# A masked attention layer on one core: the last 16 steps cut as 256 queries by two key blocks, the last tails begun sooner

## The chip, the core and the metric

The kernel runs on one core of a Trainium2 chip. A core has a matrix engine (PE, with its weight loads listed as PEld), a vector engine (DVE), an activation engine (ACT), a general engine (POOL) and a queue engine that only starts transfers (SP). Each engine works through its own list of instructions in order; they meet at semaphores. SBUF is the on-chip memory with 128 partitions, PSUM the small memory into which PE writes. The metric is the device time of one execution in microseconds (us), lower is better.

## The reference

Input `x` is (8, 2048, 256): 8 graphs of 2048 nodes with 256 channels. `adj` is one 2048 x 2048 adjacency matrix for all graphs. For each graph (H = 8 heads of D = 32):

```python
q, k, v = split(x @ w_qkv)                       # each (8, 2048, 8 heads, 32)
scores = einsum('fnhd,fmhd->fhnm', q, k) / sqrt(32)
attn = softmax(where(adj > 0, scores, -1e9), axis=-1)
t = einsum('fhnm,fmhd->fnhd', attn, v)
u = layernorm(x + t, ln1_g, ln1_b)
h = relu(u @ w1 + b1)
w = layernorm(u + h @ w2 + b2, ln2_g, ln2_b)
out = layernorm(x + w)                            # no gain, no shift
```

All of it is float32.

## The kernel before

**Steps.** The work is cut into 1024 items `(f, qc, g, mb)`: graph f (8), chunk of 512 queries qc (4), group of four heads g (2), block of 128 keys mb (16). Sixteen items with the same (f, qc, g) are a group. The main loop (L606) takes one step per item. In step t the program writes, in this order: what the planner has to fill in (`advance`), the exponential of item t+1 (`exponentials`, ACT), the scores of item t+2 (`scores`: four matmuls on PE into two PSUM tiles, then two additions of the mask on DVE, L233, which also move the scores to SBUF), the product of item t with V (`values`, four matmuls on PE, L249, summed in PSUM over the group), and what becomes of the finished tile p of item t (`add_up`). So DVE works about one item ahead of ACT, and ACT one ahead of PE's second product. "Step t" in this document means the 1024 items in order, 0 to 1023, and T(t) is the time at which L249 of item t starts. The last graph is steps 896 to 1023, the last group 1008 to 1023.

**PSUM.** Three score tiles in rotation, two of them for each item, hold the scores; two more banks hold the running product of a group and whatever the planner fills in. PE can write the scores of an item only when DVE has emptied the tile.

**Softmax sums.** The sum over keys is taken by adding p tiles: in a group POOL adds those of blocks 3, 6, 8, 10, 12, 14 into block 0 (L271), accumulating transfers started by POOL (L268) add others, and the four tiles left go through PE with a matrix of ones (`denominator`, L315). For the last group `denominator` starts three steps before the end and takes eight tiles.

**Tails.** When the two head groups of a query chunk are done, `outcome` transposes the products and divides them by the sums (`divide`, L356), adds x by an accumulating transfer that POOL starts (L340), and starts `tail`: `norm`, `feed_forward` (transposes, two matrix products, L54), `norm`, multiplication by the gain and addition (POOL, L368 and L370), a second accumulating transfer of x (L373), `norm`, and the store (SP). `norm` is four statistics instructions with their aggregates on DVE (L278, L279), four small instructions on POOL that end with the bias `nb` (L283 to L287), and four scalings on ACT (L290). Its argument `per` says how many of the four are put into one step; it is 1 for all tails but the last two. In the last graph the tails of chunks 0 and 1 begin at `begin + 10`, where `begin` is six steps after the chunk's last item.

**Planner.** Each piece of filling is a Python generator that yields at the points where it may be put off; `start(t, gen, due)` names the first step and the step at which it is due. The list is ordered by due step. Filling that needs PE asks for a PSUM bank (`BANK`), one at a time, and gets it when a credit, refilled in every step, is large enough or the piece is due; `MORE` holds the bank for another part and `WAIT` holds it idle. All of this happens when the program is built: on the chip each engine's order is fixed.

**The end.** After the last step the planner runs in its finishing mode: one request for a bank per round, the list still ordered by due step. `finish` (L443) takes the last chunk: `divide`, and then its rows in two halves (`half_rows`, L396), which take turns. What is still open of chunk 2's tail comes in between.

The planner's loop, which decides who gets the bank:

```python
        for e in list(fill):
            while e[2] is not None and e[0] <= t and e is not state["holder"]:
                if e[2] == BANK:
                    if not free or not more():
                        break
                    free = False
```

Of the kernel before, what the change touches and what calls it, by code (L numbers as in the profile page):

```python
# [16 lines left out]
ALU = mybir.AluOpType  # L17
# [44 lines left out]
def fast_path(ctx, tc, cst, x, adj, out, RS):  # L62
# [155 lines left out]


    PT, O, OT, RC, DT = {}, {}, {}, {}, {}  # L220

    def scores(item):
        f, qc, g, mb = item
        pt = PT[item] = pp.tile([P, 4, CH], F32, name="p")
        ps2 = [score_pair() for _ in range(2)]

        for half in (1, 0):
            for j in range(2):
                r = D * (2 * half + j)
                nc.tensor.matmul(ps2[half][:, j, :], KT[f, mb // TPC, g][r:r + D, (mb % TPC) * P:(mb % TPC + 1) * P],  # L230
                                 QT[f, qc, g][r:r + D, :], start=True, stop=True)
        for half, ps in enumerate(ps2):
            nc.vector.tensor_tensor(pt[:, 2 * half:2 * half + 2, :], ps,  # L233
                                    MK[f, qc, mb // 2][:, mb % 2, None, :].to_broadcast([P, 2, CH]), ALU.add)
# [6 lines left out]
    def values(item):  # L241
        f, qc, g, mb = item
        grp = (f, qc, g)
        if mb == 0:
            i = state["side"]
            O[grp] = ps_x[i].tile([P, CH], F32, name=f"x{i}")
        for h in range(4):
            r = D * h
            nc.tensor.matmul(O[grp][r:r + D, :], V[f, mb // TPC, g][:, mb % TPC, r:r + D], PT[item][:, h, :],  # L249
                             start=(mb == 0), stop=(mb == LAST))  # L250
        if mb == LAST:
            OT[grp] = op.tile([P, CH], F32, name=f"oT{g}")
            nc.scalar.copy(OT[grp], O.pop(grp))
# [6 lines left out]

    ENDED = MB - 5
    SUM = 4

    def add_up(item):
        f, qc, g, mb = item
        for chain in MOVED:
            if mb in chain[1:] and not ((f, qc, g) == items[-1][:3] and mb >= ENDED):
                nc.gpsimd.dma_start(PT[f, qc, g, chain[0]], PT.pop(item), accum_op=ALU.add)  # L268
        if mb in POOLED[1:] and not ((f, qc, g) == items[-1][:3] and mb >= ENDED):
            first = PT[f, qc, g, POOLED[0]]  # L270
            nc.gpsimd.tensor_tensor(first, first, PT.pop(item), ALU.add)  # L271


    def norm(t, per=1):
# [22 lines left out]
    def denominator(f, qc, g, ready):  # L297
        grp = (f, qc, g)
        blocks = [ALONE, MOVED[0][0], POOLED[0], MOVED[1][0]]
        late = {2: ready - 1, 3: ready}  # L300
        if (f, qc, g) == items[-1][:3]:
            blocks = [POOLED[0], 11, 12, MOVED[0][0], 13, 14, MOVED[1][0], 15]
            late = {n: len(items) - k for n, k in ((2, 2), (3, 1), (4, 1), (5, 0), (6, 0), (7, 0))}
        yield BANK
# [26 lines left out]
        begin = items.index((f, qc, g, LAST)) + SUM + 2  # L331
        start(begin, outcome(f, qc) if (f, qc) != (F - 1, NCK - 1) else finish(f, qc), begin)

    def outcome(f, qc):
# [3 lines left out]
        y = yp.tile([P, TPC, C], F32, name="y")  # L338
        yield from divide(f, qc, y)
        nc.gpsimd.dma_start(y, xin, accum_op=ALU.add)  # L340
        begin = items.index((f, qc, 1, LAST)) + SUM + 2
        if (f, qc) == (F - 1, NCK - 2):
            xb = take([P, TPC, C], F32)
            nc.sync.dma_start(xb, xin)
            start(begin + 8, tail(f, qc, y, xin, 2, xb), begin + 11)
        else:
# [13 lines left out]
    def tail(f, qc, y, xin, per=1, xb=None):  # L360
# [5 lines left out]
        z = y  # L366
        yield from norm(z, per)
        nc.gpsimd.tensor_tensor(z, z, rows(cst["g2r"]), ALU.mult)  # L368
# [26 lines left out]

    def half_rows(h, y, xr, xb, yT, hT, dst):  # L396
        own = slice(2 * h, 2 * h + 2)
        q = slice(2 * h * P, 2 * (h + 1) * P)
        y, xr, xb = y[:, own], xr[:, own], xb[:, own]

        def row2(v):
            return v[:, None, :].to_broadcast([P, 2, C])

        nc.vector.tensor_tensor(y, y, xr, ALU.add)
        if h:
            yield
        found = half_stats(y)
        yield
        half_norm(y, *found)
        nc.gpsimd.tensor_tensor(xr, y, row2(cst["g1r"]), ALU.mult)  # L410
        nc.gpsimd.tensor_tensor(xr, xr, row2(cst["be1b2r"]), ALU.add)  # L411
        yield
        ps = bank()
        transposes(ps, [y[:, j, a * P:(a + 1) * P] for a in range(2) for j in range(2)])
        for a in range(2):
            nc.scalar.activation(yT[:, a, q], ps[:, a * 2 * P:(a + 1) * 2 * P], AF.Identity,
                                 bias=cst["be1c"][:, a:a + 1], scale=cst["g1c"][:, a:a + 1])
        yield
        ps = bank()
        for d in range(2):  # L420
            for a in range(2):
                columns(ps[:, d * 2 * P:(d + 1) * 2 * P], w1s[:, a, d * P:(d + 1) * P], yT[:, a, q], start=(a == 0), stop=(a == 1))
            nc.scalar.activation(hT[:, d, q], ps[:, d * 2 * P:(d + 1) * 2 * P], AF.Relu, bias=cst["b1s"][:, d:d + 1], scale=1.0)  # L423
        yield
        ps = bank()
        for j in range(2):
            for d in range(2):
                columns(ps[:, j * C:(j + 1) * C], hT[:, d, (2 * h + j) * P:(2 * h + j + 1) * P], w2s[:, d, :],
                        start=(d == 0), stop=(d == 1))
        z = y  # L430
        nc.vector.tensor_tensor(z, ps.rearrange("p (b c) -> p b c", c=C), xr, ALU.add)
        found = half_stats(z)
        yield
        half_norm(z, *found)
        yield
        nc.vector.tensor_tensor(z, z, row2(cst["g2r"]), ALU.mult)  # L436
        nc.vector.tensor_tensor(z, z, xb, ALU.add)  # L437
        found = half_stats(z)
        yield
        half_norm(z, *found)  # L440
        nc.sync.dma_start(dst[:, own], z)

    def finish(f, qc):  # L443
        y = yp.tile([P, TPC, C], F32, name="y")
        xr, xb = state["rows"]
        yield from divide(f, qc, y)
        yT, hT = (work.tile([P, 2, CH], F32, name=n) for n in ("turned", "hT"))
        dst = out[f, qc * CH:(qc + 1) * CH, :].rearrange("(p j) c -> p j c", p=P)
        both = [half_rows(h, y, xr, xb, yT, hT, dst) for h in range(2)]
        while both:  # L450
            for e in list(both):
                if next(e, both) is both:
                    both.remove(e)
            yield 1

# [39 lines left out]
    def start(t, gen, due):  # L495
        fill.append([t, gen, 1, due])
        fill.sort(key=lambda e: e[3])
# [108 lines left out]
    for t, (f, qc, g, mb) in enumerate(items):  # L606
        if g == 1 and mb % 2 and (f + 1 < F or qc + 1 < NCK):
            load_mask(f + (qc + 1) // NCK, (qc + 1) % NCK, mb // 2)
        for what, *which in NEXT.get(t % FRAME, []):
            to = f if what is ask and which[0] else f + 1  # L610
            if to < F:
                at = (0, 0, 0) if what is turn else (which[0], 0, 0) if what is ask else (0, which[1], which[0] * TPC)
                start(t, what(to, *which), t + 3 * MB if what is turn else items.index((to, *at)) - LEAD - 1)
        if t == len(items) - MB // 2:
            xr, xb = state["rows"] = [take([P, TPC, C], F32) for _ in range(2)]
            nc.sync.dma_start(xr, x[f, qc * CH:(qc + 1) * CH, :].rearrange("(p j) c -> p j c", p=P))
        if t == len(items) - 2:
            nc.gpsimd.tensor_tensor(xb, xr, rows(cst["be2r"]), ALU.add)
# [14 lines left out]
        if mb == LAST and t + 1 < len(items):  # L633
            start(t + 2, denominator(f, qc, g, t + SUM), t + SUM + 4)
        if t == len(items) - 3:
            start(t, denominator(f, qc, g, t), t)
    t = len(items)
# [244 lines left out]
```

## Time and profile before

| what | value |
|---|---|
| median of three runs | 3190.41 us (3189.46 to 3194.38) |
| the profiled execution, whole | 3196.28 us |
| its span (first to last instruction) | 3194.5 us |
| busy share PE, DVE, POOL, ACT | 96%, 86%, 81%, 76% |
| last L249 starts, step 1023 | 3146.17 us |
| from there to the end of the span | 48.3 us |

The profile is one execution. Busy times add up the instructions of an engine; a line of the timeline gives start, length, engine, source line, operation, output and inputs, and in brackets how long the engine had been idle and what ended that. Where the timeline joins several records of one kind, `x8` says how many: a float32 matmul leaves two records, so the four matmuls of one `values` are x8. T(t) is found by counting the groups of L249 back from the last one. The profiled execution is 1.8 us longer than its span.

### The profile page before, as it was taken

How to read it: one execution, taken by the hardware profiler on the slowest of the kernel's cores; microseconds unless marked ns; L12 is line 12 of the kernel's file. 1: busy time of each engine (PE TensorE's matmuls, PEld its weight loads, DVE VectorE, ACT ScalarE, POOL GpSimd, SP SyncE). 2: the span in 40 equal slices, each digit the busy share in tenths (PEclk: the TensorE clock that was granted, in tenths of full speed). 3: DMA queues.
4: the chain of work that ended last, by engine and by line, in shares of the span. 5: the costliest groups of instructions: out<-in, count | busy, mean ns of one | idle time of the engine just before them, and what ended most of it. 6: DMA issues, size and time to landing. Idle time of an engine off the chain costs nothing. (4 is left out here: it accounts for less than half of the span.)

```text
span 3194.5 us, 68226 instructions
## 1 busy us (share of the span) xinstructions
PE 3081.7 (96%) x28868; PEld 963.0 (30%) x28868; DVE 2749.6 (86%) x3139; ACT 2417.7 (76%) x1909; POOL 2593.3 (81%) x1361
## 2 busy tenths in 40 slices
PE   7899999999999999999999999999999999999985
PEld 4222333222332223332333323323233233332222
DVE  4798988888889988889988988988988888889985
ACT  3677778777787777788777788778778778777774
POOL 0578888788888888888888888888889788889875
PEclk8899999999999999999999999999999999999998
DMA  9688889788798888898888899888879788888872
GB/s 323 142 192 193 183 175 199 161 188 189 179 195 188 191 194 178 176 204 196 187 177 174 194 208 198 168 182 196 196 174 203 177 196 192 176 177 166 178 150 64
DMA packets 153096, 589.46 MB, mean 185 GB/s; under 512 B 15024, under 2 KB 67760, under 8 KB 103888
## 3 DMA queue, kind: packets, MB, share of 16 engines
q0 software_dynamic: 64128, 433.22, 68.8%
q1 hardware_dynamic: 87840, 150.50, 13.7%
q8 instruction: 228, 3.74, 0.4%
q10 hardware_dynamic: 816, 1.31, 0.1%
q14 instruction: 84, 0.69, 0.1%
HBM read 146.67 MB, written 37.75 MB: 58 GB/s over the span
## 5 line engine op out<-in xcount | busy, mean ns | idle before, releaser
L233 DVE TENSOR_TENSOR p<-s,mask 128x1024 f32<-128x1024 f32 x2048 | 2409.1, 1218 | 325.0 <-PE s L230 182.9
L237 ACT ACTIVATE p<-p 128x2048 f32<-128x2048 f32 x1024 | 1956.0, 1910 | 566.5 <-DVE p L233 481.1
L271 POOL TENSOR_TENSOR p<-p 128x2048 f32<-128x2048 f32 x382 | 1875.4, 4909 | 359.1 <-ACT p L237 358.8
L230 PE MATMUL s<-qT,kT 32*128 32x512 f32 x8192 | 1172.5, 642 | 44.2 <-DVE p L233 39.4
L249 PE MATMUL x<-p,v 128*32 128x512 f32 x8192 | 1093.5, 606 | 4.6 <-ACT p L237 4.6
L230 PEld LDWEIGHTS s<-qT,kT 32*128 32x128 f32 x8192 | 320.9, 183 | 671.3 <-DVE p L233 643.6
L268 POOL DMA_DIRECT2D p<-p x382 | 416.8, 1092 | 70.1 <-ACT p L237 46.4
L249 PEld LDWEIGHTS x<-p,v 128*32 128x32 f32 x8192 | 161.5, 108 | 784.0 <-issue 310.2
L315 PE MATMUL x<-p,halves 128*32 128x512 f32 x2080 | 269.9, 595 | 0.0
L54 PE MATMUL x<-in,wqkv 128*32 128x512 f32 x1888 | 245.7, 592 | 0.0
L290 ACT ACTIVATE y<-y,nb,rs 128x256 f32<-128x256 f32 x372 | 219.1, 591 | 6.1 <-POOL nb L287 5.9
L278 DVE BATCH_NORM_STATS2 st<-y 128x6 f32<-128x256 f32 x372 | 155.0, 417 | 1.8 <-POOL y L370 1.8
L54 PE MATMUL x<-turned,w1s 128*32 128x512 f32 x992 | 123.9, 593 | 0.0
L54 PE MATMUL x<-w2s,hT 128*32 128x256 f32 x2016 | 121.8, 382 | 0.0
L54 PEld LDWEIGHTS x<-wqkv,in 128*32 128x32 f32 x3584 | 102.2, 110 | 64.1 <-issue 55.9
L54 PE MATMUL x<-wqkv,in 128*32 128x128 f32 x3584 | 117.4, 273 | 0.0
L315 PEld LDWEIGHTS x<-p,halves 128*32 128x32 f32 x2080 | 67.9, 111 | 156.9 <-issue 155.5
L368 POOL TENSOR_TENSOR y<-y,g2r 128x1024 f32<-128x1024 f32 x31 | 101.6, 3278 | 6.4 <-ACT y L290 6.4
L54 PEld LDWEIGHTS x<-in,wqkv 128*32 128x32 f32 x1888 | 61.3, 110 | 141.3 <-issue 116.5
L284 POOL TENSOR_TENSOR rs<-rs,mhalf 128x4 f32<-128x4 f32 x93 | 96.3, 1035 | 7.8
L370 POOL TENSOR_TENSOR y<-y,be2r 128x1024 f32<-128x1024 f32 x30 | 94.6, 3155 | 0.4
L54 PEld LDWEIGHTS x<-w2s,hT 128*32 128x32 f32 x2016 | 65.9, 111 | 70.7 <-issue 38.5
(121 smaller groups left out, 1301.1 us busy)
## 6 DMA issues: line engine op xcount, KB each, us to landing
p<-p POOLq DMA_DIRECT2D x382, 1024.0 KB, 10.0
in<-xd SPq DMA_DIRECT2D x87, 512.0 KB, 8.9
mask<-md SPq DMA_DIRECT2D x248, 128.0 KB, 8.6
y<-in_x_dram POOLq DMA_DIRECT2D x61, 512.0 KB, 10.1
p<-in_adj_dram SPq DMA_DIRECT2D x16, 1024.0 KB, 9.3
out_dram<-y SPq DMA_DIRECT2D x31, 512.0 KB, 6.2
in<-in_x_dram SPq DMA_DIRECT2D x30, 512.0 KB, 10.6
xd<-in SPq DMA_DIRECT2D x28, 512.0 KB, 8.8
```

Source lines behind the costliest of these rows:

```text
L54: nc.tensor.matmul(out[r:r + D], lhsT[:, r:r + D], rhs, start=start, stop=stop)
L230: nc.tensor.matmul(ps2[half][:, j, :], KT[f, mb // TPC, g][r:r + D, (mb % TPC) * P:(mb % TPC + 1) * P], QT[f, qc, g][r:r + D, :], start=Tr ...
L233: nc.vector.tensor_tensor(pt[:, 2 * half:2 * half + 2, :], ps, MK[f, qc, mb // 2][:, mb % 2, None, :].to_broadcast([P, 2, CH]), ALU.add)
L237: nc.scalar.activation(PT[item], PT[item], AF.Exp, scale=1.0 / math.sqrt(D))
L249: nc.tensor.matmul(O[grp][r:r + D, :], V[f, mb // TPC, g][:, mb % TPC, r:r + D], PT[item][:, h, :], start=(mb == 0), stop=(mb == LAST))
L268: nc.gpsimd.dma_start(PT[f, qc, g, chain[0]], PT.pop(item), accum_op=ALU.add)
L271: nc.gpsimd.tensor_tensor(first, first, PT.pop(item), ALU.add)
L278: nc.vector.bn_stats(st, t[:, j, :])
L284: nc.gpsimd.tensor_tensor(rs, rs, cst["mhalf"], ALU.pow)
L290: nc.scalar.activation(t[:, j, :], t[:, j, :], AF.Identity, bias=nb[:, j:j + 1], scale=rs[:, j:j + 1])
L315: nc.tensor.matmul(ps[r:r + D, :], cst["halves"][:, g, :], term[:, h, :], start=(n == 0), stop=(n == len(blocks) - 1))
L368: nc.gpsimd.tensor_tensor(z, z, rows(cst["g2r"]), ALU.mult)
```

## The change

The last group (`ENDING`) keeps its 16 steps, but a step takes 256 queries by two key blocks where it took 512 queries by one. The first eight steps finish the first 256 queries, the last eight the second 256. Scores, values and sums have their own branch for it: eight score matmuls of 256 columns in place of four of 512, the same two mask additions over the same number of elements, eight value matmuls of 256. Of each half's eight p tiles POOL adds two, one accumulating transfer adds a third, and five go through PE.

`closing(h)` replaces `finish`, `half_rows` and the special case of `denominator`: it takes the sums, the division and the whole tail of one half. It is started five steps into each half, `closing(0)` with due step 1024 and `closing(1)` with 1025, through the planner like other filling.

The other tails of the last graph are moved too. Chunks 0 and 1 begin at `begin + 7` in place of `begin + 10`, due at `begin + 18` in place of `begin + 26`, and put two statistics or scalings into a step where they put one; the second `norm` of the last graph's tails puts all four into one step. The multiplication by the second gain waits for step 15, 0 or 1 of a group (`CALM`). Chunk 2 adds x on DVE from the tile loaded by SP, in place of the accumulating transfer, and its tail begins at `begin + 3` in place of `begin + 8`.

```diff
+    ENDING = (F - 1, NCK - 1, 1)
+    HQ = CH // 2
     def scores(item):
...
+        if item[:3] == ENDING:
+            h, k = divmod(mb, MB // 2)
+            for b in range(2):
+                m = 2 * k + b
+                for half in (1, 0):
+                    for j in range(2):
+                        r = D * (2 * half + j)
+                        nc.tensor.matmul(ps2[half][:, j, b * HQ:(b + 1) * HQ],
+                                         KT[f, m // TPC, g][r:r + D, (m % TPC) * P:(m % TPC + 1) * P],
+                                         QT[f, qc, g][r:r + D, h * HQ:(h + 1) * HQ], start=True, stop=True)
...
     def add_up(item):
         f, qc, g, mb = item
+        if item[:3] == ENDING:
+            h = mb // (MB // 2) * (MB // 2)
+            if mb - h in (2, 4):
+                first = PT[f, qc, g, h]
+                nc.gpsimd.tensor_tensor(first, first, PT.pop(item), ALU.add)
+            elif mb - h == 3:
+                nc.gpsimd.dma_start(PT[f, qc, g, h + 1], PT.pop(item), accum_op=ALU.add)
+            return
+    CALM = (15, 0, 1)
     def outcome(f, qc):
...
-        yield from divide(f, qc, y)
-        nc.gpsimd.dma_start(y, xin, accum_op=ALU.add)
         begin = items.index((f, qc, 1, LAST)) + SUM + 2
         if (f, qc) == (F - 1, NCK - 2):
             xb = take([P, TPC, C], F32)
             nc.sync.dma_start(xb, xin)
-            start(begin + 8, tail(f, qc, y, xin, 2, xb), begin + 11)
+            yield from divide(f, qc, y)
+            yield 1
+            nc.vector.tensor_tensor(y, y, xb, ALU.add)
+            start(begin + 3, tail(f, qc, y, xin, 2, xb), begin + 18)
+            return
+        yield from divide(f, qc, y)
+        nc.gpsimd.dma_start(y, xin, accum_op=ALU.add)
+        if f == F - 1:
+            start(begin + 7, tail(f, qc, y, xin, 2), begin + 18)
         else:
             start(begin + 10, tail(f, qc, y, xin), begin + 26)
     def tail(f, qc, y, xin, per=1, xb=None):
...
-        yield from norm(z, per)
+        yield from norm(z, per if per == 1 else TPC)
+        while xb is None and f == F - 1 and state["now"] % MB not in CALM:
+            yield 1
+    def closing(h):
+        f, qc, g = ENDING
+        own, part, t0 = slice(2 * h, 2 * h + 2), slice(h * HQ, (h + 1) * HQ), len(items) - MB // 2 * (2 - h)
+        terms = [(5, 6), (1, 7), (0, 7), (6, 8), (7, 8)]
...
+        yield BANK
+        ps = bank()
+        for n, (block, when) in enumerate(terms):
+            if n:
+                yield MORE
+            while state["now"] < t0 + when:
+                yield WAIT
+            term = PT.pop((*ENDING, block + h * MB // 2))
+            state["credit"] -= 4 * CH
+            for b in range(2):
+                for i in range(4):
+                    r = D * i
+                    nc.tensor.matmul(ps[r:r + D, 0:HQ], cst["halves"][:, g, :], term[:, i, b * HQ:(b + 1) * HQ],
+                                     start=(n + b == 0), stop=(n + b == len(terms)))
+        dT = DT[f, qc]
+        nc.vector.tensor_tensor(dT[:, part], ps[:, 0:HQ], dT[:, part], ALU.add)
...
+        yield BANK
+        po = bank()
+        transposes(po, [OT[f, qc, gg][:, part][:, j::2] for gg in range(2) for j in range(2)])
...
+        for d in range(2):
+            yield BANK
+            ps = bank()
+            for a in range(2):
+                columns(ps[:, 0:HQ], w1s[:, a, d * P:(d + 1) * P], yT[:, a, part], start=(a == 0), stop=(a == 1))
...
-        if t == len(items) - 3:
-            start(t, denominator(f, qc, g, t), t)
+        for h in range(2):
+            if t == len(items) - MB // 2 * (2 - h) + 4:
+                start(t + 1, closing(h), len(items) + h)
```

The rest of `closing` is `half_rows` with the planner's yields (`BANK`, `MORE`, steps) between its parts, and the load of the last chunk's x, a single one in the order of the two halves, is moved to the start of the last group.

## The prediction

> **What bounds the kernel now.** I read the page first: the engines' busy shares and the groups with what ended their idle time.
>
> ```profile
> span 3194.5 us, 68226 instructions
> PE 3081.7 (96%) x28868; PEld 963.0 (30%) x28868; DVE 2749.6 (86%) x3139; ACT 2417.7 (76%) x1909; POOL 2593.3 (81%) x1361
> L233 DVE TENSOR_TENSOR p<-s,mask 128x1024 f32<-128x1024 f32 x2048 | 2409.1, 1218 | 325.0 <-PE s L230 182.9
> L230 PEld LDWEIGHTS s<-qT,kT 32*128 32x128 f32 x8192 | 320.9, 183 | 671.3 <-DVE p L233 643.6
> ```
>
> PE and DVE hand the score tiles to each other: the mask additions wait for PE's scores (182.9 us), the score loads for DVE to empty a tile (643.6 us). A step is as long as the longer of the two. The timeline of PE and DVE prices the steps of the last graph, as distances between starts of L249:
>
> - two mask additions and nothing else: 2.5 us;
> - with four more matmuls of 512 columns on PE: 2.92 us (here 2962.50 to 2965.42);
> - with twice that: 3.79 us;
> - with two statistics on DVE and no filling on PE: 3.33 us (3082.07 to 3085.40).
>
> ```profile
> 2962.50 1.06 PE L249 MATMUL x<-p,v 128*32 128x512 f32 x8
> 2963.38 1.04 PE L315 MATMUL x<-p,halves 128*32 128x512 f32 x8
> 2964.35 1.14 PE L230 MATMUL s<-qT,kT 32*128 32x512 f32 x8
> 2965.42 1.06 PE L249 MATMUL x<-p,v 128*32 128x512 f32 x8
> ...
> 3082.07 1.06 PE L249 MATMUL x<-p,v 128*32 128x512 f32 x8
> 3084.33 1.14 PE L230 MATMUL s<-qT,kT 32*128 32x512 f32 x8 [1.19 <-DVE p L233]
> 3085.40 1.07 PE L249 MATMUL x<-p,v 128*32 128x512 f32 x8
> ```
>
> A step that PE fills with four matmuls therefore has 0.42 us of room on DVE, about one statistics pair (0.42 us, L278). Two lie beyond the room, and so does a second lot of matmuls. That is the scale on which I weigh the moved tails.
>
> Then the timeline where the change works. At step 1009 ACT stood 5.60 us for POOL's `nb`, which sat behind an addition of two p tiles (5.43 us); PE then waited 4.64 us. Steps 1008 to 1011 took 3107.71 − 3091.67 = 16.04 us where three steps at 2.92 take 8.8.
>
> ```profile
> 3091.86 5.43 POOL L271 TENSOR_TENSOR p<-p 128x2048 f32<-128x2048 f32 x1
> 3099.06 0.19 POOL L287 TENSOR_SCALAR nb<-nb 128x4 f32<-128x4 f32 x1
> 3099.29 1.09 ACT L290 ACTIVATE y<-y,nb,rs 128x256 f32<-128x256 f32 x2 [5.60 <-POOL nb L287]
> 3102.23 1.60 PE L249 MATMUL x<-p,v 128*32 128x512 f32 x8 [4.64 <-ACT p L237]
> ```
>
> Last the end. The last product starts at 3146.17; 48.3 us follow. Of these PE is busy less than half up to 3170, at half clock between 3160 and 3170 (granted 0.50); the chain decides, not an engine.
>
> ```profile
> 3160.84 1.09 ACT L394 ACTIVATE y<-y,nb,rs 128x256 f32<-128x256 f32 x2 [11.99 <-issue]
> 3163.54 1.94 PE L54 MATMUL s<-turned,w1s 128*32 128x256 f32 x16 [0.66 <-ACT turned L416]
> 3171.32 3.38 PE L54 MATMUL x<-w2s,hT 128*32 128x256 f32 x32
> 3174.53 1.04 PE L54 MATMUL s<-turned,w1s 128*32 128x256 f32 x16
> ```
>
> **The change part by part.** The planner runs at build time, so I followed the changed program's order on each engine. It is the old one up to about step 939. I give the shift of T(t) against before, in the profiled execution's own time (3196.28 us whole, 5.87 above the median).
>
> *Chunk 0's first norm, three steps sooner: +4.9.* POOL starts the transfer that adds x at 2890.99; the page's group of that transfer has 10.1 us to landing, the two of the last graph 9.0 and 9.7. It lands at 2900.7. In the new order two statistics stand right behind the mask addition that ends at 2895.6, and the next addition, which ran at 2896.07, is queued behind them.
>
> ```profile
> 2890.99 0.87 POOL L340 DMA_DIRECT2D y<-in_x_dram  x1 [0.90 <-DVE y L356]
> 2893.22 2.36 DVE L233 TENSOR_TENSOR p<-s,mask 128x1024 f32<-128x1024 f32 x2 [0.27 <-PE s L230]
> 2896.07 2.36 DVE L233 TENSOR_TENSOR p<-s,mask 128x1024 f32<-128x1024 f32 x2 [0.50 <-PE s L230]
> 2899.00 2.36 DVE L233 TENSOR_TENSOR p<-s,mask 128x1024 f32<-128x1024 f32 x2 [0.57 <-PE s L230]
> ```
>
> It starts at 2900.7 + 0.95 = 2901.6, 5.5 late; PE waits for the tile, ACT for DVE. Two later statistics of before are already done (−0.6). Bounds: 3 (landing after 9.0, the 0.5 us gaps on DVE absorbed) to 5.5. Chunk 1 makes the same move without the wait: started at 2977.80 it lands by 2987.5, its statistics come at 2988.2.
>
> *The feed-forwards in lumps, steps 944 to 961: +3.5 (1 to 5).* Two steps with 8 matmuls of 512 and two with 16 of 256 take the place of eight with half as many: 4 × 3.79 + 4 × 2.5 = 25.2 against 8 × 2.92 = 23.4, +1.8. The second norm's four statistics fall into one step: 2.5 + 4 × 0.42 = 4.2 against four that each fitted beside 2.92: +1.3. Four scalings in one step (4 × 0.58 and an exponential of 1.91, 4.2 us) cost some 0.4, as ACT is ahead by most of a step.
>
> *Steps 961 to 976: +1.1 (0 to 2.5).* Chunk 1's first norm in pairs, one pair of 0.84 beyond the room, and a little more. *Steps 976 to 993: +2.4 (0.5 to 4).* Chunk 1's lumps (+1.8), its four statistics in a step, part of them beside PE.
>
> *Steps 993 to 1008: +4.7 (2.5 to 6.5).* Eight statistics in two lots (3.4) and chunk 2's addition of x, now on DVE (twice 512 elements, 0.68 each in L356: 1.3), minus the 0.42 that each of three filled steps has to spare: 3.4; before spent 1.7 there on its two steps of 3.33. Two steps running with four scalings each: 2 × (4 × 0.58 + 1.91) = 8.5 against 5.4, +3.1.
>
> *Steps 1008 to 1011: −7.2 (−8 to −5).* The gain's product now waits for a step of `CALM`, so the `nb` that was late comes at step 1002, not behind an addition of p. Nothing else is late there in the new order: four halves of 512 columns in each step, 2.92. This is the gain of the change.
>
> *The last group, steps 1011 to 1023: −1.2 (−3 to +2).* Before 38.46 us. After: twelve steps with PE filling at about 2.92 (w1s, w2s, then the first half's five sums), 35.0, plus four statistics in step 1017 (1.7) and 0.6 of ACT. The price of the 256-wide form is unknown: at one price per column it is nil, which the row supports (w2s at 256 is 382 ns, 512 wide 593 to 642, some 40 ns of it fixed); by 382 against half of 642 it would be 0.06 us × 8 records, 0.5 a step. The mask is cut into 256-element pieces; the same 1024 elements are charged.
>
> *The tail: +3.7 (−4 to +7).* In the order on PE only the first half's sums and one set of transposes stand before the last product. Behind it stand the first half's oT transposes, its y transposes, w1s, w1s, w2s, and only then the 40 matmuls of the second half's sums. Counted from T(1023): product 1.0, transposes to 1.7, two divisions, x, statistics (0.8 + 0.7 + 1.2) to 4.4, POOL's root and `nb` 1.6, scaling 1.1: 7.1. Transposes and the first `turned` to 9.5, w1s twice at the slow clock (1.94) to 13.4, hT 0.45, w2s at 3.38 to 17. The second half's sums, 40 × 0.12 = 4.8, to 22. Its sum, transposes, division and first norm take the same 6.4 as above: 28.4. From its transposes on I take what before shows for its second half, norm finished to the end: the w1s at 3174.53 to 3194.5 is 20.0, and 3.6 for transposes and `turned` ahead of it. 28.4 + 23.6 = 52.0 against 48.3.
>
> At the clock rule and trace meet. The row: after the 4.64 us of idling above the product took 1.60 instead of 1.06, and in the tail PE was slow from 3161.5 to about 3174.5, w2s in the middle included. The Trainium skill, TensorE: Matmul & The Clock Gate, Part 1, has full speed back after about 3.4 us of sustained work; by it w2s would already be fast, and the tail some 1.5 us shorter. I stay with the row, since its gaps will be in the new tail too.
>
> The other rule: the same page, section "LDWEIGHTS (loading the stationary operand)", prices a load by its columns, so 16 score loads of 128 columns in place of 8 would be 1.7 us, an estimate, against 1.14 of scores, and nine PE-filled steps some 5 us longer. The row says no: eight loads of 183 ns stand within 0.31 us, side by side.
>
> Sum: 4.9 + 3.5 + 1.1 + 2.4 + 4.7 − 7.2 − 1.2 + 3.7 = +11.9; 3196.28 + 11.9 = 3208.2, and as a median 3208.2 − 5.9 = 3202.3.
>
> **The rivals.**
>
> *The lumps hide (same).* If DVE and ACT are far enough ahead, what a lump costs in one step comes back in the next, and only the transfer, the stall that goes and the end count: 4.9 − 7.2 − 1.2 + 3.7 = +0.2, 3191. For it: ACT is 76% busy. Against: three score tiles let PE lead by less than a step, and the 3.33 us steps were not made up.
>
> *The first half really closes beside the steps (faster).* The mechanism is only in the tail. If the second half's sums don't stand behind the first half's feed-forward, its chain is sums to T+1, first norm at T+7.5, then 23.6: 31, 17 less than before; all in all about −9, 3181. It decides when those 40 matmuls start before T+8. Against: PE's order has them last.
>
> *A new wait for `nb` (slower still).* Two sets of `nb` in one step behind an addition of 4.55 us: ACT then waits at 991 or 1005 as it did at 1009. Price 3 to 5: 3207.
>
> That the change does nothing can hold only before step 939, where the order is the old one.
>
> **How the numbers follow.** About 0.2%, 6.4 us, is what a measurement of this kernel can tell from no change. Forecast 0.54 (own range 3194 to 3210), lumps hidden 0.20, new wait 0.17, first half closed 0.09. Same are the hidden lumps (0.17 of them) and the forecast's low end (0.04); faster is the closed half and the hidden lumps' low end (0.11); the rest is slower, 0.68. The range leaves out the closed half and the ends: 3187 to 3212.
>
> **What would show it.** Right: an idle stretch of about 5 us on DVE before statistics near 2896, ended by the transfer; T(1008) near 3108; no 5.60 us on ACT near step 1009; 40 matmuls of `halves` some 17 us after the last product; about 52 us from there to the end. Wrong: the sums of the second half directly behind the last product; the steps 944 to 1008 as long as before; a wait on `nb` in another place.

## The result and the profile after

The changed kernel took 3214.95 us (median of six, 3207.64 to 3220.71) against 3190.40 (median of six): 1.0072 times the time before, 95% interval 1.0052 to 1.0092. It is slower, as forecast, but the time lies above the range (3187 to 3212). The profiled execution took 3209.04 us, 0.8 from the forecast in its own time (3208.2). That nearness is an accident, as the stages below show.

The page of the changed kernel: the span, the engines, the groups that answer to those of before, and the groups of two waits.

```profile
span 3207.3 us, 68929 instructions
PE 3089.8 (96%) x29220; PEld 978.0 (30%) x29220; DVE 2757.6 (86%) x3146; ACT 2416.8 (75%) x1910; POOL 2588.5 (81%) x1358
L251 DVE TENSOR_TENSOR p<-s,mask 128x1024 f32<-128x1024 f32 x2016 | 2372.9, 1219 | 316.7 <-PE s L248 174.0
L248 PEld LDWEIGHTS s<-qT,kT 32*128 32x128 f32 x8064 | 316.6, 184 | 669.9 <-DVE p L251 643.8
L332 ACT ACTIVATE y<-y,nb,rs 128x256 f32<-128x256 f32 x372 | 217.3, 591 | 0.0
L320 DVE BATCH_NORM_STATS2 st<-y 128x6 f32<-128x256 f32 x372 | 154.8, 416 | 6.4 <-DMA y<-in_x_dram 5.1
```

The last two groups on the page of before:

```profile
L290 ACT ACTIVATE y<-y,nb,rs 128x256 f32<-128x256 f32 x372 | 219.1, 591 | 6.1 <-POOL nb L287 5.9
L278 DVE BATCH_NORM_STATS2 st<-y 128x6 f32<-128x256 f32 x372 | 155.0, 417 | 1.8 <-POOL y L370 1.8
```

Busy times have hardly moved. ACT's wait for `nb` is gone (5.9 us before, 0.0 now), and the statistics wait 5.1 us for a transfer that they did not wait for before.

The timeline says where. First PE and DVE at step 941, where chunk 0's first norm now stands:

```profile
2891.49 1.06 PE L282 MATMUL x<-p,v 128*32 128x512 f32 x8
2892.37 1.04 PE L54 MATMUL x<-in,wqkv 128*32 128x512 f32 x8
2898.53 2.09 PE L248 MATMUL s<-qT,kT 32*128 32x512 f32 x8 [5.12 <-DVE p L251]
2900.55 1.94 PE L282 MATMUL x<-p,v 128*32 128x512 f32 x8
...
2888.77 2.36 DVE L251 TENSOR_TENSOR p<-s,mask 128x1024 f32<-128x1024 f32 x2 [0.27 <-PE s L248]
2896.18 0.43 DVE L320 BATCH_NORM_STATS2 st<-y 128x6 f32<-128x256 f32 x1 [5.06 <-DMA y<-in_x_dram]
```

DVE stands 5.06 us for the transfer, PE 5.12 us for DVE; then the scores take 2.09 us in place of 1.14 and the product 1.94 in place of 1.06: the idle time cost PE its clock (granted 0.78 between 2890 and 2900). Next step 1001, DVE and POOL:

```profile
3078.85 2.35 DVE L251 TENSOR_TENSOR p<-s,mask 128x1024 f32<-128x1024 f32 x2
3081.11 5.00 DVE L384 TENSOR_TENSOR y<-y,in 128x1024 f32<-128x1024 f32 x1
3086.04 2.34 DVE L251 TENSOR_TENSOR p<-s,mask 128x1024 f32<-128x1024 f32 x2
...
3080.51 4.52 POOL L311 TENSOR_TENSOR p<-p 128x2048 f32<-128x2048 f32 x1 [0.29 <-ACT p L255]
```

L384 is the addition of x to chunk 2's tile, now on DVE. I had charged 1.3 us; it took 5.00, and ends 1.1 us after POOL's addition of two p tiles. Last PE after the last product (3158.74):

```profile
3160.30 0.75 PE L95 MATMUL x<-ident,oT 128*128 128x128 f32 x4 [0.49 <-ACT oT L275]
3165.74 1.39 PE L95 MATMUL x<-ident,y 128*128 128x128 f32 x4 [4.69 <-ACT y L441]
3167.79 3.64 PE L54 MATMUL s<-turned,w1s 128*32 128x256 f32 x32 [0.66 <-ACT turned L511]
3171.21 2.37 PE L54 MATMUL s<-w2s,hT 128*32 128x256 f32 x32
3173.40 4.49 PE L464 MATMUL x<-p,halves 128*32 128x256 f32 x80
...
3186.07 1.11 PE L95 MATMUL s<-ident,y 128*128 128x128 f32 x4
```

The second half's sums (L464) begin 14.7 us after the last product, behind the first half's feed-forward. The first half is not closed beside the steps.

### The profile page after: what moved, and what is told of

The parts are those of the page before. It is cut to its first block, busy times and chain, and to the rows that moved or that the text cites. A ratio compares the mean times of both kernels' runs of the same rounds, so it can differ in the third digit from the quotient of the medians.

```text
span 3207.3 us, 68929 instructions
## 1 busy us (share of the span) xinstructions
PE 3089.8 (96%) x29220; PEld 978.0 (30%) x29220; DVE 2757.6 (86%) x3146; ACT 2416.8 (75%) x1910; POOL 2588.5 (81%) x1358
## 4 chain that ended last, share of the span: by engine, by line
PE 83%; DVE 10%; DMA 2%; issue 2%; ACT 1%; POOL 1%; DVEq 0%; SPq 0%; ACTq 0%; POOLq 0%
PE s L248 31%; PE x L282 26%; PE x L54 16%; DVE p L251 7%; PE x L354 6%; PE x L95 3%; DMA in<-in_x_dram 1%; DVE st L320 1%; DVE dT L360 1%; PE s L236 0%; PE x L270 0%; POOL p L311 0%; DVE y L401 0%; DMA y<-in_x_dram 0%; ACT p L255 0%
## 5 line engine op out<-in xcount | busy, mean ns | idle before, releaser
L251 DVE TENSOR_TENSOR p<-s,mask 128x1024 f32<-128x1024 f32 x2016 | 2372.9, 1219 | 316.7 <-PE s L248 174.0
L311 POOL TENSOR_TENSOR p<-p 128x2048 f32<-128x2048 f32 x378 | 1850.7, 4896 | 371.4 <-ACT p L255 370.9
L248 PE MATMUL s<-qT,kT 32*128 32x512 f32 x8064 | 1157.6, 644 | 52.9 <-DVE p L251 48.3
L282 PE MATMUL x<-p,v 128*32 128x512 f32 x8064 | 1078.3, 607 | 2.6 <-ACT oT L286 1.5
L308 POOL DMA_DIRECT2D p<-p x378 | 409.7, 1084 | 67.8 <-ACT p L255 43.4
L354 PE MATMUL x<-p,halves 128*32 128x512 f32 x2016 | 261.5, 592 | 0.0
L332 ACT ACTIVATE y<-y,nb,rs 128x256 f32<-128x256 f32 x372 | 217.3, 591 | 0.0
L54 PE MATMUL x<-turned,w1s 128*32 128x512 f32 (+1 forms) x1008 | 125.0, 593 | 0.0
```

The source lines that it names most:

```text
L54: nc.tensor.matmul(out[r:r + D], lhsT[:, r:r + D], rhs, start=start, stop=stop)
L332: nc.scalar.activation(t[:, j, :], t[:, j, :], AF.Identity, bias=nb[:, j:j + 1], scale=rs[:, j:j + 1])
L354: nc.tensor.matmul(ps[r:r + D, :], cst["halves"][:, g, :], term[:, h, :], start=(n == 0), stop=(n == len(blocks) - 1))
```

## The experiments

**How the runs are read.** In all profiles T(938) differs, from 2882.7 to 2890.9 us, though the order up to there is the same in every kernel: the first product starts 96 to 103 us into the span, and at steps 175 and 187 PE waits a varying time for the input's transfer. From step 938 on the steps repeat within a few tenths of a us (the first wait for chunk 0's transfer within 0.8). So I take T(t) less before's T(t), less that difference at step 938, and give the growth by stage; "tail" is what follows T(1023), less before's 48.3. All in us.

| stage | predicted | changed | start_10 | due_26 | both | add_sooner | relu_first | old_tails | best |
|---|---|---|---|---|---|---|---|---|---|
| 938 to 944 | +4.9 | +6.8 | +0.5 | +7.3 | +0.5 | +7.4 | +7.6 | 0.0 | +0.5 |
| 944 to 961 | +3.5 | +5.3 | +5.1 | +0.5 | +0.9 | +4.7 | +4.5 | 0.0 | +0.9 |
| 961 to 976 | +1.1 | +1.1 | +0.2 | +1.0 | -0.2 | +1.1 | +1.1 | 0.0 | -0.2 |
| 976 to 993 | +2.4 | +3.7 | +4.0 | +0.5 | +1.0 | +3.6 | +3.6 | 0.0 | +1.0 |
| 993 to 1008 | +4.7 | +8.1 | +8.5 | +4.3 | +4.3 | +4.6 | +8.2 | +3.0 | +1.0 |
| 1008 to 1011 | -7.2 | -7.2 | -7.2 | -7.2 | -7.2 | -7.2 | -7.2 | -7.2 | -7.2 |
| 1011 to 1023 | -1.2 | -0.8 | -0.8 | +0.3 | +0.3 | +1.6 | -0.8 | +7.3 | +3.0 |
| tail | +3.7 | +0.2 | -0.3 | -0.4 | +1.6 | -3.1 | -10.2 | -5.9 | -10.6 |
| sum | +11.9 | +17.2 | +10.0 | +6.2 | +1.1 | +12.7 | +6.8 | -2.9 | -11.7 |

**The spread: again, again_2, again_3, again_4.** The changed kernel unedited.

> The changed kernel once more, nothing edited. Its six times so far lie in two groups, 3207.6 to 3211.1 and 3218.8 to 3220.7. Theory A: the 11 us between them arise before step 939, where both kernels have the same order, at waits for a transfer like those at steps 175 and 187 (in before's profile PE waits 4.1 us for the input at step 175, in the changed one it does not); then a profile of the upper group has T(936) 5 to 11 us later than 2879.7, and the same shifts as the first profile from there on. Theory B: they arise in the moved tails or at the end; then T(936) is 2879.7 within 1 us and a later step is longer by 5 to 11. In a profile of the lower group again, the addition of x to chunk 2 takes 5.0 us on DVE (POOL's addition of two p tiles beside it ends just before), and DVE stands 5 us for chunk 0's transfer at step 941.

> The changed kernel as it is, one more profile, to catch an execution of the upper group (3218 to 3221). If it is one: theory A, T(938) is 5 to 11 us later than in the first profile (2885.6) and the steps from there are as long as there; theory B, T(938) is 2882 to 2891, as in the five other profiles, and one stretch behind it is longer by 8 to 11. In an execution of the lower group: the shift from step 938 to 1023 against before is +17.0 within 0.5.

> The changed kernel, a look for an execution of the upper group (3218 to 3221). Theory A: T(938) is 5 to 11 us above 2885.6; theory B: T(938) is 2882 to 2891 and one stretch behind it is longer by 8 to 11. In the lower group: +17.0 from step 938 to 1023 within 0.5, and a whole of 3207 to 3214.

> The changed kernel, one more look for the upper group, with the same two theories and numbers as for again_3.

The first took 3207.56 to 3213.51 in four executions (median 3211.9; ratio 1.0060, 1.0043 to 1.0077), the others 3212.37, 3210.61 and 3213.45. From step 938 to 1023 all four profiles have +16.9, and T(938) moves by 2 to 5 us against the first one. That is theory A for the spread inside the lower group. No profile fell into the upper group: three of the first six executions, none of these seven. Where its 10 us arise stays open.

**quarter_add.** The addition of x to chunk 2 on a quarter of the elements.

```diff
-            nc.vector.tensor_tensor(y, y, xb, ALU.add)
+            nc.vector.tensor_tensor(y[:, 0:1], y[:, 0:1], xb[:, 0:1], ALU.add)
```

> The addition of x to chunk 2's tile on DVE works on 256 of the 1024 elements per partition; the rest of x is left out there, so chunk 2 of the last graph comes out without three quarters of that sum. Theory: DVE waited for POOL's addition of two p tiles to end, since both read two operands from SBUF; then it still takes about 4 to 4.6 us (5.00 less 0.5 to 1.0 for the elements), ends within 0.7 us of the end of POOL's addition, and step 1001 stays 7 to 8.1 us long. Rival: the 5.00 us are the cost of 1024 elements in this form; then it takes a quarter, about 1.25 us, and step 1001 falls by some 4 us, to 4.

The timeline of this run, DVE and then POOL:

```profile
3082.45 4.20 DVE L384 TENSOR_TENSOR y<-y,in 128x256 f32<-128x256 f32 x1
...
3081.85 4.52 POOL L311 TENSOR_TENSOR p<-p 128x2048 f32<-128x2048 f32 x1 [0.29 <-ACT p L255]
```

4.20 us for a quarter of the elements; it ends at 3086.65, 0.28 after POOL's addition (3086.37). When it began, 3.92 us of POOL's addition were left. So about 3.9 us are waiting and not work. The rival falls.

**add_sooner.** The same addition, one step sooner.

```diff
             yield from divide(f, qc, y)
-            yield 1
             nc.vector.tensor_tensor(y, y, xb, ALU.add)
```

> The yield between chunk 2's division and the addition of its x is dropped, so the addition stands on DVE one step sooner, right behind the division (at 3078.85 in the first profile of the changed kernel), where POOL's addition of two p tiles ends 0.6 us later and the next one begins 1.7 us later. Theory of the shared access: the instruction takes 1.2 (its elements, by 4.20 against 5.00 and by 0.69 for 512) plus at most 0.6 of waiting, under 2.2 us in place of 5.00; the stretch from step 1000 to 1008 gets 3.5 to 5 us shorter, and no half clock on PE at step 1001. Rival (a fixed cost of this instruction, whatever POOL does): 4 us or more again. The end moves with it, to 3 to 5 us sooner.

DVE and POOL of this run:

```profile
3076.77 1.54 DVE L383 TENSOR_TENSOR y<-y,in 128x1024 f32<-128x1024 f32 x1
...
3072.66 4.56 POOL L311 TENSOR_TENSOR p<-p 128x2048 f32<-128x2048 f32 x1 [1.90 <-ACT p L255]
3078.32 4.52 POOL L311 TENSOR_TENSOR p<-p 128x2048 f32<-128x2048 f32 x1 [0.29 <-ACT p L255]
```

POOL's one addition ends 0.45 us after the start, and the next, which waited for ACT, begins as DVE is done: 1.54 us. The three times are what is left of POOL's addition and an own time: 3.92 + 1.08 in the changed kernel, 3.92 + 0.28 for a quarter of the elements, 0.45 + 1.09 here. Steps 993 to 1008 cost 4.6 in place of 8.1. The gain reaches the end: the sum is 4.5 lower (3205.51, ratio 1.0045, 1.0031 to 1.0060), with steps 1011 to 1023 2.4 longer and the tail 3.3 shorter.

The Trainium skill, SBUF — State Buffer, section "Who interferes with whom", says that a DVE instruction with two inputs in SBUF shares its second read with a GpSimd instruction that reads SBUF, and that whichever is issued second blocks until the first is finished. The changed kernel and both runs agree with it where DVE is second (5.00 and 4.20 behind POOL, 1.54 almost clear of it); a GpSimd addition held up by DVE is not seen here. The mask additions have one input in PSUM and show no such wait: 1.22 us beside the same additions.

**start_10.** Only the start of chunks 0 and 1 put back.

```diff
-            start(begin + 7, tail(f, qc, y, xin, 2), begin + 18)
+            start(begin + 10, tail(f, qc, y, xin, 2), begin + 18)
```

> Chunks 0 and 1 of the last graph begin their tails at begin + 10 again, all else as changed. Theory: the wait of 5.06 us for chunk 0's transfer at step 941 goes, so the shift between steps 936 and 944 falls from +6.8 to about +0.5; with the due step still at 18 the feed-forward is as lumped as before, +5 to +7 between 944 and 961, and the end is 4 to 8 us earlier than in the changed kernel, the ratio to before about 1.004. Rival (the statistics wait for something else, or the time is lost later again): within 2 us of the changed kernel.

938 to 944 falls from +6.8 to +0.5, every other stage stays within 1 us, the sum falls by 7.2 (3205.09, ratio 1.0039, 1.0025 to 1.0054). The wait for the transfer, with the clock that it costs, was all but 0.5 us of the first stage.

**due_26.** Only the due step of chunks 0 and 1 put back.

```diff
-            start(begin + 7, tail(f, qc, y, xin, 2), begin + 18)
+            start(begin + 7, tail(f, qc, y, xin, 2), begin + 26)
```

> Chunks 0 and 1 of the last graph are due at begin + 26 again, all else as changed. Theory of the lumps: the feed-forwards are spread by the credit again, steps of 2.92 in place of 3.79, which gives back 1 us in each of eight steps (952 to 955, 984 to 987) and perhaps 1 to 2 for two runs of four scalings: the end 5 to 10 us earlier. Rival (lumps are made up in the next steps): within 2 us.

3198.50 us, ratio 1.0025 (1.0013 to 1.0037); the sum is 11 lower, a little more than expected. Of this 8.0 lie in the two stages of the feed-forwards (944 to 961 and 976 to 993) and 3.8 in steps 993 to 1008, where chunk 1's last norm no longer stands beside chunk 2's first. PE of the changed kernel with the lumps, then of this run:

```profile
2932.86 1.06 PE L282 MATMUL x<-p,v 128*32 128x512 f32 x8
2933.75 1.90 PE L54 MATMUL x<-turned,w1s 128*32 128x512 f32 x16
2936.65 1.07 PE L282 MATMUL x<-p,v 128*32 128x512 f32 x8
```

```profile
2932.84 1.06 PE L282 MATMUL x<-p,v 128*32 128x512 f32 x8
2933.73 1.04 PE L54 MATMUL x<-turned,w1s 128*32 128x512 f32 x8
2935.77 1.06 PE L282 MATMUL x<-p,v 128*32 128x512 f32 x8
```

3.79 us from product to product with 16 records of `w1s`, 2.93 with 8. The due step decides that, the only edit of this run: once it is past, the planner hands over matmuls without asking for credit.

**both.** The two together.

> Chunks 0 and 1 begin at begin + 10 and are due at begin + 26, as before the change; pairs in a step, the four at once in the second norm, CALM, chunk 2 and the last group stay as changed. Theory that the two costs are separate and add: the shift between step 938 and the last step falls from +17.0 by 6.7 (start_10) and 10.4 (due_26) to 0, and with 48.5 behind it the end is within 2 us of before in a profile counted from step 938. Rival: with a later start the due step takes hold less, or the lumps meet chunk 2's tail: a shift of +4 or more, or the stall on nb at step 1009 comes back (+7).

The sum is +1.1 where 17.2 − 7.2 − 11.0 gives −1.0: the two add up within some 2 us, which lie in the tail (+1.6). 3191.96 us, ratio 0.9996 (0.9985 to 1.0008), no difference that can be told. What is left of the change then costs about what it gains.

**sums_first.** `closing` pauses the first half, so that the second half's sums come first.

```diff
         nc.gpsimd.tensor_tensor(xr, xr, row2(cst["be1b2r"]), ALU.add)
+        if h == 0:
+            yield 2
         yield BANK
```

> The changed kernel with one pause in closing(0): its y transposes wait two rounds, so PE takes the second half's 40 matmuls of sums directly behind the first half's oT transposes, and the second half's transposes next. Nothing before the last product moves. Theory (the second half's chain sets the end, and its sums stand in the queue behind the first half's feed-forward, from 14.7 us after the last product): the sums then begin 2 us after the last product and end at 6.5, the second half's first norm is done at 13 in place of 27, its y transposes follow the first half's w2s at 14, and the end comes 33 to 37 us after the start of the last product in place of 48.6: 12 to 15 us sooner. Rival (the first half's chain, or the one engine behind both, sets the end): less than 4 us.

A miss: the tail was 45.65 us, not 33 to 37 (whole 3210.10, ratio 1.0053, 1.0034 to 1.0071). PE and ACT of this run:

```profile
3165.08 4.52 PE L464 MATMUL x<-p,halves 128*32 128x256 f32 x80
3171.76 1.96 PE L54 MATMUL x<-turned,w1s 128*32 128x256 f32 x32 [0.65 <-ACT turned L513]
3179.03 1.08 PE L54 MATMUL s<-w2s,hT 128*32 128x256 f32 x8 [5.31 <-ACT hT L521]
3188.15 1.94 PE L54 MATMUL s<-turned,w1s 128*32 128x256 f32 x16 [3.42 <-ACT turned L513]
...
3176.54 1.09 ACT L441 ACTIVATE y<-y,nb,rs 128x256 f32<-128x256 f32 x2 [4.38 <-DVE nb L439]
3177.54 1.07 ACT L332 ACTIVATE y<-y,nb,rs 128x256 f32<-128x256 f32 x2
3178.52 0.45 ACT L521 ACTIVATE hT<-x,b1s 128x256 f32<-128x256 f32 x1
```

The sums moved as meant, but a new wait took the place of the old one: on ACT the first half's relu (L521) is queued behind the second half's norm (L441), which waits 4.38 us for its bias, and behind chunk 2's scalings (L332).

**relu_first.** On top of `sums_first`, ACT's order is mended, by pauses in `closing` and in chunk 2's last `norm`.

```diff
-        yield 1
+        yield 3 if h else 1
         half_norm(y, *found)
...
         found = half_stats(z)
-        yield 1
+        yield 1 if h else 2
         half_norm(z, *found)
...
-    def norm(t, per=1):
+    def norm(t, per=1, gap=2):
...
-        yield 2
+        yield gap
...
-        yield from norm(z, per)
+        yield from norm(z, per, 2 if xb is None else 7)
```

> sums_first with the order on ACT mended: the second half's first norm waits two rounds more, so that the first half's two relus stand before it on ACT, the first half's second norm one round more, and chunk 2's last four scalings stand behind these. In sums_first PE waited 5.31 us for the first half's relu (it stood behind the second half's norm and chunk 2's scalings on ACT), and the second half's turned rows stood behind the first half's second norm (3.4 us). Theory (those two waits took the gain of sums_first back): the tail from the last product to the end is 35 to 39 us in place of 45.7, the steps before are as in sums_first. Rival (the chain of the halves through POOL and DVE alone is that long): 43 us or more.

The tail is 38.17 us, and the whole 3199.40 (ratio 1.0020, 1.0009 to 1.0032). PE:

```profile
3172.75 1.96 PE L54 MATMUL x<-turned,w1s 128*32 128x256 f32 x32 [0.66 <-ACT turned L513]
3174.52 0.61 PE L54 MATMUL s<-w2s,hT 128*32 128x256 f32 x8
3175.30 1.50 PE L54 MATMUL s<-w2s,hT 128*32 128x256 f32 x24 [0.16 <-ACT hT L521]
3179.88 1.09 PE L54 MATMUL s<-turned,w1s 128*32 128x256 f32 x16 [0.54 <-ACT turned L513]
```

PE does not wait for the first relu, where it waited 5.31 us, and 0.16 us for the second. Without the long waits the clock stays up: 16 records of the second half's `w1s` take 1.09 in place of 1.94. (The first half's 32 records, 3.64 in the changed kernel, took 1.96 in `sums_first` already, right behind the sums.) So PE's order and ACT's order set the tail together; mending one alone gave 3 of 10 us.

**no_calm, chunk2_8, chunk2_8_no_calm, old_tails.** Which edit took away the stall at step 1009? Each starts from `both`: without `CALM`; with chunk 2 at `begin + 8`; with both edits undone; and with one statistic to a step besides.

```diff
-        while xb is None and f == F - 1 and state["now"] % MB not in CALM:
-            yield 1
...
-            start(begin + 3, tail(f, qc, y, xin, 2, xb), begin + 18)
+            start(begin + 8, tail(f, qc, y, xin, 2, xb), begin + 18)
...
-            start(begin + 10, tail(f, qc, y, xin, 2), begin + 26)
+            start(begin + 10, tail(f, qc, y, xin), begin + 26)
```

> both without CALM: the product with the second gain no longer waits for step 15, 0 or 1. In POOL's list the last nb of chunk 1 then again stands directly behind an addition of two p tiles at the end of the group before the last, as before the change. Theory (CALM is what took the stall at step 1009 away): steps 1008 to 1011, or the two before, lose 4 to 7.3 us more than in both, and the whole is that much later. Rival (the stall went for another reason, the new last group for example): within 2 us of both.

> both with one number put back: chunk 2's tail begins at begin + 8 in place of begin + 3; CALM stays. no_calm has shown that CALM did not take the stall at step 1009 away. Theory: chunk 2's sooner first norm did; put back, its nb stands on POOL behind the last addition of p tiles of the group (4.5 us) and behind the product with the gain (2.4 to 3.3), and ACT waits for it again: steps 1008 to 1011 take 13 to 18 us in place of 8.8, the whole 4 to 9 us more than both. Rival (the last group's own order, with fewer additions on POOL, took it away): within 2 us of both.

> The same without CALM: to be held against no_calm, which differs only in begin + 3. The nb then stands directly behind the last addition of p tiles, with no product ahead of it. Theory: steps 1008 to 1011 take 11 to 16 us, 2 to 7 more than in no_calm. Rival: within 2 us of no_calm.

> both with the three edits undone that could have taken the stall at step 1009 away, all at once: chunks 0 and 1 put one statistic or scaling into a step again, no CALM, and chunk 2's tail begins at begin + 8. What is left of the change is the new last group with its closing and chunk 2's addition on DVE. Around the last group POOL has the order of before: product with the gain, addition of p tiles, second product, two transfers, addition of p tiles, then nb. Theory (each of the edits alone clears POOL in time, so undoing one or two of them, as in no_calm, chunk2_8 and chunk2_8_no_calm, shows nothing): the stall is back, steps 1008 to 1011 take 14 to 17 us in place of 8.8. Rival (the new last group took it away): 8.8 to 11 us.

All four theories fell. Steps 1008 to 1011 took 8.8, 8.8, 9.6 and 8.8 us (times: 3194.08, 3198.90, 3199.55, 3194.41; ratios 1.0002, 1.0008, 1.0019, 0.9991, all within 0.003 of 1). The sums of the stages are +1.4, +2.2, +3.8 and -2.9, so without `CALM` and with chunk 2's tail at `begin + 8` the profiled execution lost 0.3 and 1.1 us against `both`, and not by the stall. In `old_tails` POOL's order around the place is that of before, and yet ACT waits 0.94 us for `nb` and not 5.60:

```profile
3097.53 1.10 ACT L332 ACTIVATE y<-y,nb,rs 128x256 f32<-128x256 f32 x2 [0.94 <-POOL nb L329]
...
3090.34 5.19 POOL L311 TENSOR_TENSOR p<-p 128x2048 f32<-128x2048 f32 x1
3097.30 0.19 POOL L329 TENSOR_SCALAR nb<-nb 128x4 f32<-128x4 f32 x1
```

POOL of before where the lists part, then of `old_tails`:

```profile
3070.05 0.88 POOL L340 DMA_DIRECT2D y<-in_x_dram  x1 [1.33 <-DVE y L356]
3070.64 4.88 POOL L271 TENSOR_TENSOR p<-p 128x2048 f32<-128x2048 f32 x1
```

```profile
3068.45 4.85 POOL L311 TENSOR_TENSOR p<-p 128x2048 f32<-128x2048 f32 x1
```

Against before, `nb` comes 1.8 us sooner and ACT reaches its scalings 2.9 later (3096.6 to 3093.7); together that is the difference between 5.60 and 0.94. Up to this `nb` POOL's list differs from before in one place only: the transfer that added x to chunk 2 is gone, for which POOL had waited 1.33 us, and the next addition of p begins 2.2 us sooner. POOL's first addition of the new last group begins at 3100.50, behind this `nb`, so that group did not make `nb` sooner. ACT is later because the addition of x on DVE (2.48 us here) holds the steps up by 3.1 us between 1001 and 1002. So in this run the move of that addition took the stall away, and 3.0 of the 7.2 us only changed their place, to steps 993 to 1008. That none of the other three edits was needed for it is shown; that one of them would be enough without the move to DVE was not tried.

In `old_tails` the new last group stands almost alone: +7.3 in steps 1011 to 1023 and -5.9 in the tail, 1.4 us lost. The sum of -2.9 comes from the stall.

**best.** `both`, `add_sooner` and `relu_first` in one.

> All edits that gave something: begin + 10 and due + 26 for chunks 0 and 1, chunk 2's addition one step sooner, and the closing order of relu_first. If the parts add: the last product at the shift of both (-0.4) less 1 to 4 for the addition, and a tail of 35 to 39 in place of 48.3: 11 to 17 us sooner than before, ratio 0.9948 to 0.9966. If the later tails of chunks 0 to 2 now collide with the closing (in both the tail was 49.9, 1.3 longer than in the changed kernel): 6 to 10 sooner.

PE of this run, from the last product (3138.90) to the second half's y transposes:

```profile
3138.90 1.94 PE L270 MATMUL x<-p,v 128*32 128x256 f32 x16
3141.33 5.32 PE L463 MATMUL x<-p,halves 128*32 128x256 f32 x80 [0.49 <-ACT oT L275]
...
3152.79 0.94 PE L95 MATMUL s<-ident,y 128*128 128x128 f32 x4
```

The sums begin 2.4 us after the last product and the second half's y transposes 13.9 us after it, in place of 14.7 and 27.3.

3180.36 us (median of five, 3178.36 to 3184.85), ratio 0.9962 (0.9949 to 0.9976): faster than either kernel, and 12 us faster than before. The sum of the stages is -11.7, of which the tail gives -10.6 (37.70 us) and the vanished stall -7.2.

## Why the prediction was wrong, step by step

The sign and the main places were right, the size was not: from step 938 on the change cost 17.2 us, not 11.9. In the profiled execution this was hidden, since its T(938) came 4.45 us sooner than in before's. The miss of 5.3 is +8.8 in the stages before the last product and -3.5 in the tail. The time lies above the range for two reasons: this sum, and three of six executions 10 us above the rest (the ten others, seven of them taken later, have a median of 3211.0, just inside the range).

- **Chunk 0's first norm** (+4.9, measured +6.8). The wait was right: 5.1 predicted, 5.06 measured. Left out was the clock: 0.95 on the scores and 0.88 on the product behind the idle time, 1.8 in all. I had the row for it (1.60 in place of 1.06 after 4.64 us of idling) and used it in the tail alone. The same term is missing at step 957 (scores 1.99, product 1.86: 1.65 us of slow matmuls, for which DVE waited 1.03). At steps 1001 to 1002 PE was slow as well (2.09, 1.94 and 2.08: 2.8), but there it cost nothing: DVE, without a gap from 3081.1 to 3097.1, set the pace, and in `again` the third of these took 1.14 and the stage grew by the same 8.1.
- **The lumps** (+1.8 for each feed-forward; in the first one the four lump steps grew by 4.3 together). My step was "eight filled steps of 2.92 against four of 3.79 and four of 2.5". The steps that became lumps had cost 2.49 to 2.80 before, not 2.92, and of the four steps set free one gave 0.4 back. Then came the step with the four statistics and the slow clock (+2.3), and two later steps gave 0.4 and 0.9 back.
- **Steps 993 to 1008** (+4.7, measured +8.1). The term that failed is "twice 512 elements at 0.68, so 1.3": the addition took 5.00, 3.7 more. L356, from which the 0.68 came, has one of its inputs in PSUM, and it takes 0.68 beside POOL's addition as well; the new addition has both in SBUF. POOL and DVE of before:

```profile
3063.29 4.57 POOL L271 TENSOR_TENSOR p<-p 128x2048 f32<-128x2048 f32 x1
3066.21 0.68 DVE L356 TENSOR_TENSOR y<-x,rc 128x512 f32<-128x512 f32 x1
```

A lot of four statistics took 2.13 us, 0.53 for each with its aggregate, where I had counted 0.42 for the first instruction of the pair alone: 0.9 more for the two lots. Against that, two steps of four scalings took 7.13 and not 8.5. With these three the sum would have been 4.7 + 3.7 + 0.9 − 1.4 = 7.9.

- **The stall** (-7.2, measured -7.2). The size was right, the reason not: I named `CALM`, and without it the stall stays away as well. In `old_tails`, without all three edits that I had thought of, the addition on DVE took it away, and 3.0 of the 7.2 reappear in the stage before. The -7.2 came true by luck.
- **The last group** (-1.2, measured -0.8). The 256-wide form is at no extra cost: eight score loads and matmuls of 256 in 1.15 us, eight values in 1.07, against 1.14 and 1.06. (By the rows of the prediction, 382 ns for 256 columns and 593 to 642 for 512, the fixed part would be 122 to 171 ns and not 40; nothing rests on it.)
- **The tail** (+3.7, measured +0.2). The order was as read, with the second half's sums last; they began 14.7 us after the last product, not 17, since `w2s` took 2.37 and not 3.38 there; from the second half's y transposes to the end it took 21.2, not 23.6. The choice of the slow row for `w2s` was wrong: behind 3.64 us of slow `w1s` PE was nearly at full speed again (32 records of `w2s` took 1.91 in the last group), the other reading that the prediction weighs.
- **The rivals.** That lumps hide fell with due_26 (8.0 us given back in the stages of the feed-forwards). That a new wait for `nb` appears did not come. That the first half closes beside the steps was not so; made true in PE's queue alone it gave 3 us, with ACT's queue 10, not the 17 that I had worked out without ACT's order.

## What to carry to other kernels

Price a stall as the wait and the clock behind it, but only where PE sets the pace: at steps 941 and 957, 1.7 to 1.8 us of slow matmuls came on top of waits of 2 to 5 us, and at step 1001 2.8 us of them were hidden behind DVE. An instruction moved from a transfer to DVE is to be priced by where its operands lie and by what POOL does at that moment, not by the duration of an instruction with other operands. A chain moved forward in one engine's queue has to be followed through the queue of the next engine, or the wait only changes its place.

## What the runs showed of the hardware that I had not expected

- Two inputs in SBUF on DVE beside an addition on POOL: the time is what is left of POOL's instruction and about 1.1 us for 1024 elements: 5.00 with 3.92 left, 2.48 with 1.39 left (`old_tails`), 1.54 with 0.45 left; 4.20 for 256 elements with 3.92 left. The profile shows the waiting as busy time of DVE.
- PE's clock fell behind waits of a little over 2 us too, but not behind all: in the ten profiles that have the wait of 2.28 us at step 957, the next two groups of matmuls were slow (scores 1.24 to 1.99, product 1.86 to 1.94); behind the same wait at step 989 only two of the ten were slow; behind 2.23 us in `add_sooner` PE was at full speed. The changed kernel, then `add_sooner`:

```profile
2950.12 1.99 PE L248 MATMUL s<-qT,kT 32*128 32x512 f32 x8 [2.28 <-DVE p L251]
```

```profile
3079.50 1.14 PE L248 MATMUL s<-qT,kT 32*128 32x512 f32 x8 [2.23 <-DVE p L251]
```
